# Cross-attention in a decoder layer: the target mask as a scale, five query projections as seven half-size products, and one mask loaded later

## The chip, the cores and the metric

The kernel runs on one core of a Trainium2 chip. The time is the device time of one execution in microseconds (us); below it stands as the median of several runs. A core has five engines, each of which takes its own instructions in order: TensorE (PE: matrix products, with PEld for the loading of weights), VectorE (DVE), ScalarE (ACT), GpSimd (POOL) and SyncE (SP, which here only issues transfers). They wait for each other through semaphores. PE writes its products to PSUM, a small memory of eight banks; DVE and ACT read them from there.

## What is computed

One decoder layer in float32, for 8 positions of 512 rows with 512 features each. Relative-position self-attention over the 8 positions comes first, with a layer norm; then cross-attention to a context of 512 rows with 1024 features, with a layer norm; then a feed-forward layer with 2048 hidden features rounded to an 8-bit format, and a layer norm. The change touches the cross-attention:

```python
src_trans = einsum('bsf,of->bso', src, W_src) + b_src
tgt_trans = einsum('btf,of->bto', tgt, W_tgt) + b_tgt
src_trans = src_trans * src_mask[:, :, None]
tgt_trans = tgt_trans * tgt_mask[:, :, None]
k, v = split(src_trans)            # 8 heads of 64
q = tgt_trans                      # 8 heads of 64
scores = einsum('bthd,bshd->bhts', q, k) / sqrt(64)
scores = where(src_mask[:, None, None, :] == 0, -inf, scores)
attn = softmax(scores, axis=-1)
tgt_update = einsum('bhts,bshd->bthd', attn, v)
out = einsum('btf,of->bto', concatenate([tgt, tgt_update]), W_out) + b_out
```

Both masks are the same array: one row of 512 zeros and ones for each of the 8 positions. A query row whose mask is zero has all scores equal, so its softmax is the plain mean over the unmasked keys.

## The kernel before

The kernel has two parts. The first part does the self-attention for four groups of 128 rows. The order of its products on PE is planned by costs written into the code (`must`, `fill`, `slot`), and between them it works off the projection of the context into keys and values for positions 0 to 5, a generator called `context_work`. These projections use a scheme for 2 x 2 blocks of matrices that needs seven half-size products instead of eight, after Strassen and Winograd; it needs sums of the weight blocks (`sums_of_a`) and of the data blocks (`steps_of_b`). In the same generator `sum_w1` loads blocks of the feed-forward weights `w1`, forms their sums on POOL, and `store_w1` writes them to a DRAM buffer `w1d`; load and store are issued by SP.

The second part goes round by round over the positions, `t` from 0 to 7. PE, DVE, ACT and SP follow the written order. In round `t` stand the attention of position `t`; the output projection of position `t - 1` (`output_of`, again seven products, line 1307); the closing products of the feed-forward of position `t - 2` (`finish`, four steps for four groups of rows, lines 1481 to 1491); the queries of position `t + 1` (`queries`, line 1094); and the hidden layer of position `t - 1` (`hidden_of`, seven products for each of four groups, line 1389). The list `dense` holds all but the attention, each step with a cost. `weave` sets the attention steps (scores, line 1115; attention times values, `av`, line 1216) between them, spaced by these costs.

The softmax runs beside this: `scores` queues small steps for DVE and ACT, and `run` issues some of them ahead of every PE step, in proportion to that step's cost. A score block takes a DVE step that adds the mask and finds the row's minimum (line 1130), an exponential on ACT (line 1140), a division (line 1155) and a transpose (line 1163) on DVE; 16 transfers then arrange the blocks (`move_blocks`, tiles `pb` to `pT`).

`queries` multiplies 512 columns at a time: for each of four output groups four matmuls are summed in one PSUM bank, and DVE then adds the bias and multiplies by `mq` (line 1102). `load` brings one mask row to all partitions, and POOL makes two tiles of it: `mb`, 1e30 where a key is masked, and `mq`, the mask times -1/8. PSUM has a pool of four banks (`ps_b`) for all products but the scores. `hp` is a pool of three tiles (`hs`) for the partial results of `hidden_of`. `ring` holds two slots of seven weight blocks for `hidden_of`, and between them a block of `w_xo` for `output_of`. `load_x1T` brings the input of a position, which `turn_x1` transposes on DVE.

## Time and profile before

| | |
|---|---|
| time, median of 3 runs | 2002.66 us (2002.34 to 2005.05) |
| profiled execution | 2002.95 us, of which the span is 2001.2 us |
| first part | 0 to about 865 us |
| first queries of the second part | 864.7 us |
| rounds 2 to 6 | 132 us each |
| PE busy | 1967.3 us, 98% of the span |
| DVE busy | 1582.2 us, 79% |
| ACT busy | 564.1 us, 28% |
| POOL busy | 228.3 us, 11% |

The profile is one execution as the hardware's profiler recorded it. A line of a timeline gives the start in us, the length, the engine, the line of the code, the operation, the tile written and the tile read, their shapes, and the number of instructions merged into it. In square brackets stands the idle time before it, with the work of another engine that ended it. One matmul call in float32 appears as two instructions; the length of a group includes the run-out of its last one, so the distance between the starts of groups tells the rate. Lines of stretches give, for each engine, the busy time and the number of instructions, then the clock granted to PE as a share of the full clock, the share of time in which the transfer engines were busy, and GB/s. Lines of waits give the waiting engine, tile and line, what it waited for, the total in us, how often, and the longest.

### The profile page before, as it was taken

Reading aid. Unit: us, or ns where it says so; the run is one execution under the profiler, and the core shown is the slowest. Engines: PE = TensorE matmul, PEld = TensorE weight load, DVE = VectorE, ACT = ScalarE, POOL = GpSimd, SP = SyncE. Lnnn points to the kernel's source line nnn. Section 1 sums busy time; section 2 is a strip of 40 time slices with the busy share of each in tenths; the row PEclk is TensorE's granted clock in tenths of the full one; section 3 lists DMA queues with packets and bytes.
Section 4 is the critical chain, followed back from the end, with each engine's and each line's share of the span. In section 5 each row is a group of like instructions: output and inputs, shape, how many; then the busy total and the mean of one; then the engine's idle time right before and its main releaser. Section 6 shows DMA issues by size and latency. Waiting matters only on the chain.

```text
span 2001.2 us, 20415 instructions
## 1 busy us (share of the span) xinstructions
PE 1967.3 (98%) x6936; PEld 1108.4 (55%) x6936; DVE 1582.2 (79%) x2485; ACT 564.1 (28%) x1226; POOL 228.3 (11%) x232
## 2 busy tenths in 40 slices
PE   9999999998999999999999999999999999999998
PEld 4544444444444444443456657566576575676776
DVE  4999999999899989656796785877958868678443
ACT  2111111120111011123235245253252442535322
POOL 0030022002301121122101001002010010000000
PEclk9999999999999999999999999999999999999999
DMA  6635136251342352678598667776877676855621
GB/s 227 226 116 219 42 114 233 77 206 65 102 168 78 120 203 65 166 251 211 167 199 248 149 185 229 153 204 166 187 207 172 165 214 156 232 148 145 204 93 60
DMA packets 248104, 328.87 MB, mean 164 GB/s; under 512 B 85312, under 2 KB 140608, under 8 KB 243776
## 3 DMA queue, kind: packets, MB, share of 16 engines
q1 hardware_dynamic: 229200, 291.09, 51.2%
q10 hardware_dynamic: 17056, 29.66, 4.4%
q0 software_dynamic: 1744, 6.82, 0.9%
q8 instruction: 55, 0.90, 0.2%
q14 instruction: 49, 0.40, 0.1%
HBM read 195.90 MB, written 64.49 MB: 130 GB/s over the span
## 4 chain that ended last, share of the span: by engine, by line
PE 74%; DVE 18%; issue 4%; DMA 2%; ACT 1%; POOL 1%; SPq 0%; ACTq 0%; DVEq 0%; POOLq 0%
PE hx L1389 11%; PE hz L1389 5%; PE pox L1307 5%; PE av L1216 5%; PE s L1115 5%; PE o L1481 5%; PE psq L1094 5%; PE px L697 5%; DVE sc L267 4%; PE po L355 4%; DVE pq L258 4%; PE ps_q L225 3%; PE hy L1389 3%; PE poz L1307 3%; PE ps_k L225 3%
## 5 line engine op out<-in xcount | busy, mean ns | idle before, releaser
L1140 ACT ACTIVATE pe<-pe,nmax 128x512 f32<-128x512 f32 x256 | 182.7, 715 | 190.5 <-DVE nmax L1130 160.5
L1130 DVE CUSTOM_DVE_ANT_0 pe<-s,mb 128x512 f32<-128x512 f32 x256 | 162.8, 683 | 27.5 <-PE s L1115 24.4
L1163 DVE STREAM_TRANSPOSE pb<-pe 128x512 f32<-128x512 f32 x256 | 162.2, 682 | 0.6 <-issue 0.6
L258 DVE TENSOR_TENSOR pq<-qw,k 128x2048 f32<-128x2048 f32 x64 | 152.9, 2388 | 1.2
L322 DVE TENSOR_TENSOR pv<-v,sc 128x2048 f32<-128x2048 f32 x64 | 147.0, 2297 | 6.2 <-ACT v L295 4.5
L267 DVE TENSOR_REDUCE sc<-pq 128x64 f32<-128x2048 f32 x64 | 145.9, 2280 | 1.0
L1115 PE MATMUL s<-kT,qTx 64*128 64x512 f32 x512 | 129.8, 624 | 3.4 <-DVE nmax L1130 3.2
L225 PE MATMUL ps_q<-w_in,xt 128*128 128x512 f32 x256 | 117.7, 603 | 5.2 <-DVE qw L254 5.2
L1216 PE MATMUL av<-pT,vx 128*64 128x512 f32 x512 | 118.3, 604 | 4.2 <-DMA kT<-kd 4.2
L1389 PE MATMUL hx<-x2s,w1r 128*128 128x256 f32 x512 | 119.5, 383 | 0.8 <-DVE hs L1417 0.8
L1155 DVE TENSOR_SCALAR pe<-pe,rden 128x512 f32<-128x512 f32 x256 | 116.7, 498 | 4.5
L225 PE MATMUL ps_k<-w_in,xt 128*128 128x512 f32 x256 | 115.1, 602 | 4.6 <-DMA xt<-in_xT_dram 4.6
L1389 PE MATMUL hx<-x2T,w1r 128*128 128x256 f32 x512 | 118.4, 381 | 0.6 <-ACT hs L1411 0.6
L355 PE MATMUL po<-w_o,aoT 128*128 128x512 f32 x256 | 115.3, 593 | 0.9 <-ACT aoT L371 0.9
L225 PE MATMUL ps_v<-w_in,xt 128*128 128x512 f32 x256 | 114.4, 593 | 0.1
L1481 PE MATMUL o<-w2q,hq 128*128 128x512 fp8e4 x512 | 114.4, 379 | 0.0
L1094 PE MATMUL psq<-x1Ts,w_tgt 128*128 128x512 f32 x256 | 113.8, 596 | 0.6 <-PE av L1216 0.6
L1389 PEld LDWEIGHTS hx<-x2s,w1r 128*128 128x128 f32 x512 | 95.5, 190 | 28.8 <-DVE nmax L1130 14.0
L1389 PEld LDWEIGHTS hx<-x2T,w1r 128*128 128x128 f32 x512 | 96.5, 190 | 20.6 <-issue 6.9
L1418 ACT ACTIVATE hq<-hs 128x512 fp8e4<-128x512 f32 x96 | 60.5, 630 | 145.6 <-DVE hs L1417 145.6
L697 PE MATMUL px<-tx,w 128*128 128x512 f32 x192 | 88.4, 604 | 3.6 <-DVE st L739 3.4
L365 POOL TENSOR_TENSOR r<-r,bo 128x512 f32<-128x512 f32 x32 | 48.9, 1545 | 329.7 <-DMA r<-in_x_dram 327.5
(203 smaller groups left out, 3048.9 us busy)
## 6 DMA issues: line engine op xcount, KB each, us to landing
pT<-pb SPq DMA_DIRECT2D x480, 128.0 KB, 2.4
w1r<-w1d SPq DMA_DIRECT2D x32, 1024.0 KB, 6.9
w1r<-w1d SPq DMA_DIRECT2D x32, 768.0 KB, 5.3
ch<-in_ctxT_dram SPq DMA_DIRECT2D x24, 512.0 KB, 5.8
td<-tx SPq DMA_DIRECT2D x12, 768.0 KB, 4.9
tx<-td SPq DMA_DIRECT2D x12, 768.0 KB, 7.2
r<-in_x_dram SPq DMA_DIRECT2D x32, 256.0 KB, 3.5
x1Ts<-x1d SPq DMA_DIRECT2D x32, 256.0 KB, 6.3
```

The source lines that it names most:

```text
L225: nc.tensor.matmul(ps, lhsT=xt[:, e, :], rhs=w_in[:, e, part * E : (part + 1) * E], start=(e == 0), stop=(e == EC - 1),)
L258: nc.vector.tensor_tensor(pr, qw[:, fs] .rearrange("p (h d) -> p h d", d=D1) .unsqueeze(2) .to_broadcast([P, HH, T, D1]), k_all[j][:, :, f ...
L267: nc.vector.tensor_reduce(sc[j][:, t, g * HH * T : (g + 1) * HH * T], pr.rearrange("p h s d -> p (h s) d"), AX.X, ALU.add,)
L355: nc.tensor.matmul(po, lhsT=aoT[t][:, c * P : (c + 1) * P], rhs=w_o[:, c, :], start=(c == 0), stop=(c == EC - 1),)
L697: nc.tensor.matmul(bank, lhsT=w7[:, a, f, i * P : (i + 1) * P], rhs=b[f], start=start and f == 0, stop=f == HF - 1, skip_group_check=not s ...
L1094: nc.tensor.matmul(ps, lhsT=w_tgt[:, e, o * P : (o + 1) * P], rhs=x1T[t][:, e, :], start=(e == 0), stop=(e == EC - 1),)
L1115: nc.tensor.matmul(ps[:, h, :], lhsT=qT[t, c][half[h], j * P : (j + 1) * P], rhs=kT[t, c][half[h], :], start=True, stop=True,)
L1130: nc.vector.tensor_tensor_reduce(out=pe, in0=ps[:, h, :], in1=mb[t], scale=1.0, scalar=FMAX, op0=ALU.add, op1=ALU.min, accum_out=nmax[:, h ...
L1140: nc.scalar.activation(pe, pe, AF.Exp, bias=nmax[:, h : h + 1], scale=-1.0, accum_out=den[:, h : h + 1],)
L1216: nc.tensor.matmul(av[half[h], :], lhsT=v[t, c][:, s, half[h]], rhs=pT[t, c][:, :, :, s, h].rearrange("p g i q -> p (g i) q"), start=(s == 0),
L1389: nc.tensor.matmul(banks[g, name][:, i], lhsT=w[:, f, i * P : (i + 1) * P], rhs=b[:, f], start=start and f + i == 0, stop=f == 1, skip_gro ...
L1481: nc.tensor.matmul(po, lhsT=rows_of_j, rhs=w2q[:, c, :], start=(c == 0), stop=(c == HC - 1),)
```

## The change

*The mask.* `mq` goes. The queries are no longer multiplied by the mask: `queries` only adds the bias. The DVE step on the scores takes a scale per row, `score_scale`, which is the mask times -1/8, and the sign of `mb` is turned. A masked query row then gets equal exponentials over all 512 keys, masked ones too; as masked values are zero, the division only needs a factor, `row_scale`, which is 1 for an unmasked row and 512 over the number of unmasked keys for a masked one. `count_valid` computes both once, in the setup of the first part. The mask is loaded straight into `mb`.

*The queries of positions 3 to 7* (`FIRST_HALVED`) become seven half-size products, `query_steps`. The sums of the query weights are made in `context_work` with those of `w1`: four more blocks, stored to `wtd`. Three of the sums come into free places of `ring` at the end of `output_of` (`load_wt`), and the second part of a `w1` block that stood there is loaded after the queries instead; the fourth sum takes the place of a quarter of `w_tgt` in round 1 (`load_wt3`). The sums of the data are made by `query_sum` in the `hs` tiles. The results are gathered in the query tiles by ACT (`keep`) and DVE (`add`). Between the products stand the sums for the hidden layer and its first product.

*The mask of position 1* is loaded behind the fourth step of round 0 rather than at its start.

The core of the diff:

```diff
@@ in context_work
                 blocks = [(4 * part + n, f) for n in range(4) for f in range(2)]
+                blocks += [(8 + part, f) for f in range(2)]
...
-                        if i == 1 and m < PAIRS - 1:
+                        if (i == 1 and m < PAIRS - 1) or (i == 0 and m > 0):
                             sum_w1(w7[:, 7], *blocks.pop(0))
@@ load
-            mq = mp.tile([P, S], F32, tag="mq", name=f"mq{t}")
-            nc.sync.dma_start(mq, mask[t].partition_broadcast(P))
             mb[t] = mp.tile([P, S], F32, tag="mb", bufs=2, name=f"mb{t}")
-            nc.gpsimd.tensor_scalar(mb[t], mq, 0.0, MASKED, ALU.is_equal, ALU.mult)
-            nc.gpsimd.tensor_scalar(mq, mq, -1.0 / math.sqrt(D2), None, ALU.mult)
-            return mq
+            nc.sync.dma_start(mb[t], mask[t].partition_broadcast(P))
+            nc.gpsimd.tensor_scalar(
+                mb[t], mb[t], 0.0, -MASKED, ALU.is_equal, ALU.mult
+            )
@@ queries
-            nc.vector.scalar_tensor_tensor(
-                qT[t, o], ps, col(C_BT + o), mq, ALU.add, ALU.mult
+            nc.vector.tensor_scalar(qT[t, o], ps, col(C_BT + o), None, ALU.add)
+        def query_sum(t, i):
...
+            dst, u, w = (
+                (1, b12, b11),
+                (2, b22, query_t[t, 1]),
+                (3, b22, b12),
+                (4, b21, query_t[t, 2]),
+            )[i]
+            nc.vector.tensor_tensor(query_t[t, dst], u, w, ALU.subtract)
+        def query_steps(t):
...
+            def product(name, w, b, start):
+                if start:
+                    query_bank[name] = bank(f"q{name}{t}").rearrange(
+                        "p (i q) -> p i q", i=2
+                    )
+                for f in range(2):
+                    for i in range(2):
+                        nc.tensor.matmul(
+                            query_bank[name][:, i],
+                            lhsT=w[:, f, i * P : (i + 1) * P],
+                            rhs=b[:, f],
+                            start=start and f + i == 0,
+                            stop=f == 1,
+                            skip_group_check=not (start and i == 0),
+                        )
...
+            def keep(r, c, name):
+                for i in range(2):
...
+                    nc.scalar.activation(
+                        target(r, c, i),
+                        query_bank[name][:, i],
+                        AF.Identity,
+                        bias=col(C_BT + 2 * r + i),
+                    )
+            def add(r, c, name):
+                for i in range(2):
+                    y = target(r, c, i)
+                    nc.vector.tensor_tensor(y, query_bank[name][:, i], y, ALU.add)
...
+            def y():
+                product("y", of_w(0, 1), of_x(1, 0), True)
+                keep(0, 0, "y")
+            def x():
+                product("x", of_w(0, 0), of_x(0, 0), True)
+                add(0, 0, "x")
+            def z():
+                product("z", sums_of_w(0), query_t[t, 1], True)
+                keep(1, 1, "z")
+            def x2_():
+                product("x", sums_of_w(1), query_t[t, 2], False)
+                keep(0, 1, "x")
+                query_sum(t, 3)
+            def z2():
+                product("z", sums_of_w(2), of_x(1, 1), False)
+                add(0, 1, "z")
+            def x3():
+                product("x", of_w(1, 0), query_t[t, 3], False)
+                add(1, 1, "x")
+            def x4():
+                product("x", of_w(1, 1), query_t[t, 4], False)
+                keep(1, 0, "x")
+            return sum([of(1.8, f) for f in (y, x, z, x2_, z2, x3, x4)], [])
@@ scores
-                    scale=1.0,
+                    scale=score_scale[:, t, j : j + 1],
...
-                        pe, pe, rden[:, h : h + 1], None, ALU.mult
+                        pe,
+                        pe,
+                        rden[:, h : h + 1],
+                        row_scale[:, t, js[i] : js[i] + 1],
+                        ALU.mult,
+                        ALU.mult,
@@ the rounds
-                mq = load(t + 1) if t + 1 < T else None
...
+                halved = FIRST_HALVED <= t + 1 < T
+                if 0 < t < T - 1:
+                    load(t + 1)
...
-                        3: of(0.0, convert, 1) + of(0.0, turn_v_soon, 1),
+                        3: of(0.0, convert, 1) + of(0.0, turn_v_soon, 1) + of(0.0, load, 1),
...
+                    if halved:
+                        dense += of(0.0, query_sum, t + 1, 0)
                     dense += done[2]
...
+                    if halved:
+                        dense += of(0.0, query_sum, t + 1, 1)
+                        dense += of(0.0, query_sum, t + 1, 2)
                     dense += done[3]
...
+                    if halved:
+                        dense += asked[:5] + sums[0] + sums[1] + asked[5:6]
+                        dense += steps[:1] + sums[2] + asked[6:] + sums[3]
+                        dense += of(0.0, load_w1, (t - 1) * GROUPS + 1, 1)
+                        queried = len(dense)
+                        steps = steps[1:]
+                    else:
+                        dense += asked[:-1] + sums[0] + sums[1] + asked[-1:]
+                        dense += sums[2] + sums[3]
+                        queried = len(dense)
                     dense += steps
```

## The prediction

> **What bounds the kernel now.** I read the engine table first, then the busy slices, then busy time by stretches of 200 us.
>
> ```profile
> PE 1967.3 (98%) x6936; PEld 1108.4 (55%) x6936; DVE 1582.2 (79%) x2485; ACT 564.1 (28%) x1226; POOL 228.3 (11%) x232
> PE   9999999998999999999999999999999999999998
> ...
> DVE  4999999999899989656796785877958868678443
> ...
> 1200.00:1400.00 200.00, 199.94 (x866) 133.50 (x865) 147.23 (x327) 82.55 (x191) 22.98 (x18) 1.00 0.71 188
> ```
>
> In the second half TensorE (PE) is busy 199.94 of 200 us at full clock, so a microsecond off its work, or a microsecond in which it waits, counts in full. VectorE (DVE) has 147 of 200 there, an average that hides where it lags. The timeline of one round of 132 us shows where: PE first, then DVE over the same stretch.
>
> ```profile
> 1289.21 3.63 PE L1481 MATMUL o<-w2q,hq 128*128 128x512 fp8e4 x16
> 1292.68 3.60 PE L1094 MATMUL psq<-x1Ts,w_tgt 128*128 128x512 f32 x8
> 1298.12 10.57 PE L1094 MATMUL psq<-x1Ts,w_tgt 128*128 128x512 f32 x24
> ...
> 1279.60 0.18 DVE L109 RECIPROCAL rs_b<-sd_b 128x4 f32<-128x4 f32 x1 [0.36 <-ACT sd_b L107]
> ...
> 1301.85 0.67 DVE L1068 STREAM_TRANSPOSE vx<-raw 128x512 f32<-128x512 f32 x1
> 1302.44 0.71 DVE L1102 SCALAR_TENSOR_TENSOR qTx<-psq,colv,mq 128x512 f32<-128x512 f32 x1
> ...
> 1305.28 0.74 DVE L1102 SCALAR_TENSOR_TENSOR qTx<-psq,colv,mq 128x512 f32<-128x512 f32 x1
> ...
> 1322.31 0.17 DVE L1152 RECIPROCAL rden<-den 128x2 f32<-128x2 f32 x1 [1.60 <-ACT pe L1140]
> ```
>
> The first query product ends at 1296.2, and DVE empties its bank at 1302.44: 6.2 us late. DVE does not idle from 1279.60 to 1320.7, because four closing steps (`finish`), the normalisation, the transposes and the softmax all fall here. Before, this lag is free: the four products use four banks, and PE goes on.
>
> Last, what a wait of PE costs besides itself: the timeline of PE, and the granted clock (the column after POOL's) in the stretches behind two waits.
>
> ```profile
> 172.36 5.40 PE L697 MATMUL px<-tx,w 128*128 128x512 f32 x8 [2.30 <-DVE st L739]
> 917.44 3.79 PE L1115 MATMUL s<-kT,qTx 64*128 64x512 f32 x8 [2.92 <-DVE nmax L1130]
> 968.43 5.00 PE L1216 MATMUL av<-pT,vx 128*64 128x512 f32 x16 [4.22 <-DMA kT<-kd]
> 488.54 6.06 PE L225 MATMUL ps_q<-w_in,xt 128*128 128x512 f32 x8 [5.20 <-DVE qw L254]
> ...
> 174.00:176.00 2.00, 2.00 (x4) 0.82 (x3) 1.38 (x2) 0.00 (x0) 0.00 (x0) 0.53 0.47 180
> 490.00:492.00 2.00, 2.00 (x3) 0.68 (x2) 2.00 (x3) 0.00 (x0) 0.00 (x0) 0.50 0.00 0
> ```
>
> Undisturbed, these groups take 3.60 (px, ps_q), 1.99 (s) and 3.65 us (av). After a wait of 2.30 to 5.20 us the clock is about half for some 4 us, and PE loses 1.8, 1.8, 1.35 and 2.46 us more.
>
> **The change, part by part.** The sum is made against the profiled execution: span 2001.2, time 2002.95, 0.29 over the median of 2002.66.
>
> *Seven half-size products, positions 3 to 7.* Per position, 16 matmuls of 512 columns become 28 of 256; each is two instructions. In the chain 24 psq instructions take 10.50 us (437.5 ns each) and 16 of hx 3.65 (228 ns). So 32 x 0.4375 = 14.0 us becomes 56 x 0.228 = 12.77: a gain of 1.23 us, 6.2 over five.
>
> *The waits it adds.* `y`, `x`, `z` come first, then a second product is summed into the bank of `x`. It has to wait until DVE has read the first (`add(0, 0, "x")`). Only `z`, 8 x 0.228 = 1.8 us, lies between. In the changed program's order on DVE these two adds stand behind all the work of the lag, plus three query sums. The walk, with times of the round shown:
> - PE: the order puts the output's last product after the scores, so it ends at 1278.62 rather than 1276.7. The end of `o_3` stays at 1292.7; scores 1.92 and three products 5.5 put PE at 1300.1.
> - DVE: `rs_b` comes 2.9 us after that last product, 1281.5. Then reciprocal 0.2, normalisation and transpose 1.5, closing step 2.27, three more pairs 4.4, `x1T` transposes 2.38, first query sum 0.7 (as L148), one score step 0.6, reciprocal and two divisions 1.1: 1294.7. The next division waits until ACT has loaded its table and taken the exponential (1.28 + 0.9 after the score step): 1295.9. Division 1.1, closing step 2.27, two query sums 1.4, four transposes 2.4, closing step 2.24, `vx` transpose 0.6, reciprocal 0.2, three output normalisations 1.5: 1307.6. Two adds of 256 columns (0.34 each, as L1295 at 128x256): 1308.3.
>
> PE waits 1308.3 - 1300.1 = 8.2 us. Behind it in PE's queue stand the four other query products, the hidden layer's first product and two scores: everything. The second wait is that of `x3` for ACT's `keep(0, 1)`, queued behind two exponentials and a table load: 1313.1. At full clock PE would be there at 1312.0, and wait 1.1 us.
>
> The half clock takes the 1.1 us over: with 1.35 to 2.46 us lost, I take 1.95 (the mean of the four is 1.85, and this wait is longer than any), PE reaches `x3` near 1314. So 8.2 + 1.95 - 1.23 = +8.9 us per position; the last has no `vx` transpose (0.6 less). Five: +44. Nothing gives it back: PE is full until the next round, and DVE is idle again before the next lag. Bounds: 7 to 9 us of wait and 1.35 to 2.46 of clock (upwards also the 1.1 us): +35 to +56.
>
> The Trainium skill ("TensorE: Matmul & The Clock Gate", Part 1) puts the return to full clock at about 3.4 us of sustained activity, and lets it fall only after an idle window of that length. The rows here fall already after 2.30 us. From its 3.4 us at half rate one would estimate 1.7 us a wait, 8.5 in all, against the rows' 9.8.
>
> *DVE and ACT load.* Four evictions (737 ns) give way to four sums (0.69) and six half adds (0.34): +1.9 us a round, inside the walk. ACT gets eight half evictions (467 ns), beside 28% load. The second scalar of the division and the pointer scale of the scores: one pointer costs 498 ns (L1155), two 504 to 560 (L113), so 0 to 62 ns; a gain is excluded, as nothing is taken out. I take 0; 0.4 us in the walk is its upper end.
>
> *Weights through the ring.* `load_wt` issues 768 KB as two transfers (0.38 us of SP each), some 40 us before use. Behind them on SP stand four `x1T` loads, wanted a round later. The second part of the next `w1` block goes out only after the queries; ten products (18 us) lie between it and its use, and 6.9 us is its landing. Cost 0; with that cover gone, 6.9 a position. `load_wt3` is one transfer of 256 KB, a round ahead: 0.
>
> *Sums of the query weights, first part of the kernel.* Four more blocks: 16 sums on POOL, 3.5 us a block, 14.1 us beside a POOL busy 133 of 870; eight loads and four stores on SP, where `w1d` stores waited for POOL 44.8 us in 11 cases, with `xt`, `r` and context loads behind. PE waited for a transfer once in this part (2.1 us), for DVE 5.2. So -2 to +5; I take +1. `count_valid`: one matmul (pg: 0.22 us) and six small DVE steps (about 0.18 each) in the 2.12 us that DVE idles before the first `qw`: +0.2.
>
> *Mask.* The score scale replaces `mq`; POOL loses 1.5 us a position, off the path. The mask now lands in `mb`, so SP waits until the previous position's last scores are read; behind it is a `kT` load that waited for PE until 1244.7 anyhow, 5 us after the mask's issue at 1239.5: 0. In round 0 it moves. These rows show what it held:
>
> ```profile
> 896.45 2.32 POOL L967 TENSOR_SCALAR mb<-mq 128x512 f32<-128x512 f32 x1 [26.32 <-DMA mq<-in_mask_dram]
> ...
> 903.10 0.69 ACT L179 ACTIVATE kst<-psk,colv 128x512 f32<-128x512 f32 x1 [10.74 <-DMA kd<-kst]
> ```
>
> POOL waits for the mask with the `kd` store behind it; ACT waits for that store with exponentials behind it; DVE idles 11.1 us for those; PE waits 2.92 at 917 and loses 1.8 by the clock. If all goes: -4.7. The wait at 968 (4.22 + 1.35) could go as well: -10.3; or the moved mask does the same where it is now: 0. I take -4.7, as 968 waits for other transfers.
>
> Sum: 2002.95 + 44 + 1.2 - 4.7 = 2043.5; taken as 2044.
>
> **Rivals.**
> 1. *Faster: DVE is in time.* The gains alone, 6.2 + 4.7 - 1.2, give 1993. For it: 53 us of 200 are idle on DVE, and the hidden layer's seven products, with the same bank summed four times, hardly wait, as the waits of PE say:
>
> ```profile
> PE hx L1389 <- DVE hs L1417: 0.8, 1, 0.8
> ```
>
> It decides if the adds end before PE is done with `z`, 8.2 us earlier than the walk has them. Against: no gap in 41 us of DVE; and the hidden layer puts two products and an attention product between, after the lag is worked off.
> 2. *Half the wait.* If the DVE work is shorter or PE later by some 4 us, a position costs 4 + 1.8 - 1.2 = 4.6: 2002.95 + 23 - 3.5 = 2022.
> 3. *The weights come late as well*: 3 to 7 us more a position, 2060 to 2078. Against: the cover named above.
> 4. *No difference*: gain and short waits (1.2 us a position) cancel, and round 0 keeps its wait: 2003.
>
> **How the numbers follow.** Forecast 0.72, rival 1 0.08, rival 2 0.12, rival 3 0.05, rival 4 0.03. The forecast's own range: +35 to +56, with -10.3 to 0 and -2 to +5, each not at its end at once, 2028 to 2060. Reaching to rival 2, the range is 2018 to 2060. About 0.2% (4 us) is what a measurement can tell from none. Faster 0.08; same 0.04; slower 0.88.
>
> **What would show it.** Right: among PE's waits a line of the query products for DVE `qTx`, about 8 us, five times; a granted clock near 0.5 behind each; rounds of 141 rather than 132 us; no wait at 917. Wrong: five rounds of about 131 us. I am wrong if DVE enters the stretch earlier than 1281.5, if ACT makes it wait where I have none, or if its steps with two scalars cost other than the rows I took.

## The result and the profile after

The changed kernel takes 2038.81 us (median of 4 runs, 2037.17 to 2040.1), the kernel before 2003.03 us beside it (2002.34 to 2005.05): a ratio of 1.0177, with a 95% interval of 1.0159 to 1.0194. It is 1.8% slower; the forecast was 2044 us. The profiled execution took 2039.12 us, with a span of 2037.3.

The engine table and the busy slices of TensorE (PE) in the profile after; the second fence is the row of the stretch from 1200 to 1400 us (busy time of PE, weight loads, DVE, ACT, POOL, then granted clock, DMA share and GB/s).

```profile
PE 1967.5 (97%) x7058; PEld 1137.1 (56%) x7058; DVE 1625.7 (80%) x2522; ACT 581.7 (29%) x1266; POOL 229.5 (11%) x240
...
PE   9999999998999999998999899899899898999998
```

```profile
1200.00:1400.00 200.00, 192.50 (x854) 133.33 (x855) 147.09 (x316) 85.09 (x195) 19.91 (x16) 0.98 0.71 188
```

PE's busy time has not changed in sum (1967.3 us before, 1967.5 now), though the queries are less work. The slices of the second half, all 9 before but the last, now hold 8s, and in the stretch from 1200 to 1400 us PE is busy for 192.50 in place of 199.94 us, at a mean clock of 0.98 in place of 1.00. The waits of PE say what it waits for (us in total, times, longest):

```profile
PE qx L1175 <- DVE qTx L1203: 37.0, 5, 7.5
...
PE s L1255 <- DVE nmax L1270: 3.0, 4, 1.5
...
PE hx L1535 <- DVE hs L1563: 0.8, 1, 0.8
```

The hidden layer's products wait as little as before. The four waits of the scores (`s`) lie in round 0. The line of the query products is new: the query products in bank `x` wait for VectorE's `qTx`, 37.0 us in five waits, one in each round with half-size products. Here is one such round on PE and then, from the same stretch, the end of DVE's work ahead of the add for `x` (start, length, what was done, and in brackets the idle time before it and what ended that).

```profile
1299.09 1.99 PE L1175 MATMUL qy<-x1Ts,w_tgt 128*128 128x256 f32 x8
1300.92 1.89 PE L1175 MATMUL qx<-x1Ts,w_tgt 128*128 128x256 f32 x8
1302.65 1.89 PE L1175 MATMUL qz<-qs,w1r 128*128 128x256 f32 x8
1312.04 3.78 PE L1175 MATMUL qx<-qs,w1r 128*128 128x256 f32 x8 [7.50 <-DVE qTx L1203]
1315.62 1.98 PE L1175 MATMUL qz<-x1Ts,w1r 128*128 128x256 f32 x8
1317.43 1.89 PE L1175 MATMUL qx<-qs,w_tgt 128*128 128x256 f32 x8
```

```profile
1285.89 0.18 DVE L112 RECIPROCAL rs_b<-sd_b 128x4 f32<-128x4 f32 x1 [0.37 <-ACT sd_b L110]
...
1305.98 0.66 DVE L1635 TENSOR_TENSOR o<-o,b2q 128x512 f16<-128x512 f32 x1
...
1308.23 0.71 DVE L1098 STREAM_TRANSPOSE vx<-raw 128x512 f32<-128x512 f32 x1
...
1309.04 2.28 DVE L116 TENSOR_SCALAR x<-x,mvc,rs_c 128x512 f32<-128x512 f32 x3
1311.24 0.75 DVE L1203 TENSOR_TENSOR qTx<-qx,qTx 128x256 f32<-128x256 f32 x2
```

PE is done with `z` at 1304.5 and stands until 1312.04. DVE is not idle from 1285.89 on: the closing of the last output block (from 1305.98), the transpose of the values, the reciprocal and three output normalisations all come before the two adds at 1311.24, which end at 1311.99. PE goes on 0.05 us later. The product behind the wait takes 3.78 us, the one after it 1.98. The granted clock in single microseconds:

```profile
1308.00:1309.00 1.00, 0.00 (x0) 0.00 (x0) 0.97 (x4) 0.66 (x3) 0.00 (x0) 0.98 0.96 209
1309.00:1310.00 1.00, 0.00 (x0) 0.00 (x0) 0.96 (x2) 1.00 (x3) 0.91 (x1) 0.50 0.92 195
...
1315.00:1316.00 1.00, 1.00 (x4) 0.80 (x4) 0.06 (x2) 1.00 (x5) 0.00 (x0) 0.61 0.92 205
1316.00:1317.00 1.00, 1.00 (x7) 0.87 (x5) 0.00 (x0) 1.00 (x4) 0.00 (x0) 1.00 0.94 197
```

It falls to 0.50 at 1309.0, 4.5 us after PE went idle, and is back at about 1315.8, 3.7 us after PE resumed.

A round, from the first query product of one position to that of the next, takes 139.9 us (four rounds, 1159.22 to 1718.90) in place of 132.1. The first part of the kernel, which eleven of the runs below have in common with it, ended between 863.4 and 873.3 us in their profiled executions, so the kernels are compared below also by their **second part**, from the first query product of position 0 to the end of the span, and by this **round**. Before: second part 2001.2 - 864.7 = 1136.5 us, round 132.1. After: 2037.3 - 864.0 = 1173.3 us, round 139.9. Round 0 is taken from the first query product of position 0 to that of position 2, as the queries of position 1 fall into it. Of the 36.8 us of difference, round 0 gives back 2.7 (161.2 in place of 163.9 us), and the five rounds with half-size products cost the rest.

### The profile page after: what moved, and what is told of

The parts are those of the page before. It is cut to its first block, busy times and chain, and to the rows that moved or that the text cites. A ratio compares the mean times of both kernels' runs of the same rounds, so it can differ in the third digit from the quotient of the medians.

```text
span 2037.3 us, 20787 instructions
## 1 busy us (share of the span) xinstructions
PE 1967.5 (97%) x7058; PEld 1137.1 (56%) x7058; DVE 1625.7 (80%) x2522; ACT 581.7 (29%) x1266; POOL 229.5 (11%) x240
## 4 chain that ended last, share of the span: by engine, by line
PE 72%; DVE 21%; issue 2%; DMA 2%; ACT 1%; SPq 0%; POOL 0%; ACTq 0%; DVEq 0%
PE hx L1535 11%; PE px L730 6%; PE hz L1535 5%; PE pox L1452 5%; PE s L1255 5%; PE av L1361 4%; PE po L358 4%; PE ps_q L228 3%; PE ps_v L228 3%; PE ps_k L228 3%; DVE sc L270 3%; PE pz L730 3%; PE psk L174 3%; PE hy L1535 3%; PE poz L1452 3%; DVE pq L261 2%
## 5 line engine op out<-in xcount | busy, mean ns | idle before, releaser
L1270 DVE CUSTOM_DVE_ANT_0 pe<-s,mb,score_scale 128x512 f32<-128x512 f32 x256 | 178.7, 746 | 15.9 <-PE s L1255 14.6
L1295 DVE TENSOR_SCALAR pe<-pe,rden,row_scale 128x512 f32<-128x512 f32 x256 | 132.7, 561 | 4.7
L1563 DVE TENSOR_TENSOR hs<-hz,hs 128x512 f32<-128x512 f32 x32 | 22.1, 690 | 90.8 <-PE hz L1535 87.3
```

The lines of the kernel that those rows point to most:

```text
L1270: nc.vector.tensor_tensor_reduce(out=pe, in0=ps[:, h, :], in1=mb[t], scale=score_scale[:, t, j : j + 1], scalar=FMAX, op0=ALU.add, op1=ALU ...
```

## The experiments

The theory was that of the prediction: VectorE is late at one place, and the second product in `x` is the first work of PE that has to wait for it. The rivals were other causes at the same place (weights, clock, ACT), and other parts of the change. All times are medians beside runs of the kernel before on the same chip.

### Is it VectorE's lateness? Its work left out

```diff
+            if bare:
+                if j == NJ - 1:
+                    side.append((("y", t), 1.0, lambda: None))
+                    for k in range(NJ):
+                        side.append((("y", t), 0.7, lambda k=k: put(t, k)))
+                return
             r = x1[t][:, j, :]
             nc.vector.tensor_tensor(r, r, o16, ALU.add)
             stats_of(sm, mvc[t][:, j % n, :], r, f"c{t}_{j}")
```

Here `bare` holds for positions 0 to 4; the lines behind it only store the output rows as they stand.

> The changed kernel with VectorE's residual sum, statistics, root and output normalisation left out for the first five positions (their output is then stored as it stands before these steps); the eviction of the output blocks stays, TensorE's order is unchanged, and nothing else of VectorE's or ACT's is put in their place. That takes three sums with their statistics (1.55 us each) and three normalisations with the reciprocal (2.4 us) from ahead of the add, 7.0 us, and the root that ACT's copies stood behind. Theory (VectorE is late by 7.5 us at this place, itself and through ACT's root): the wait falls to 0.5 us, 1.5 at most, and the product behind it runs at 1.9 us; 2038.8 - 5 x (7.0 + 1.8) = 1995 us, 1990 to 2003. Rival (a further engine or the exchange of the banks holds the product): waits of 3 us or more stay, 2015 us or more.

1996.7 us (ratio to before 0.997, 0.9959 to 0.9981), round 130.7, second part 1129.9. The query products' waits for DVE in the whole execution, and the place itself:

```profile
PE qx L1175 <- DVE qTx L1203: 1.0, 4, 0.3
```

```profile
1297.31 1.89 PE L1175 MATMUL qz<-qs,w1r 128*128 128x256 f32 x8
1299.45 1.99 PE L1175 MATMUL qx<-qs,w1r 128*128 128x256 f32 x8 [0.25 <-DVE qTx L1203]
```

The five waits of 7.5 us became four of 0.25, the product behind runs in 1.99 us, and 42 us are gone; 44 were expected. The round is 9.2 us shorter, which is the wait (7.25) and the clock's loss behind it (1.85). PE's products are the same in number and shape, so it is not the products, their weights or their bank: it is 7 us of work ahead of an add. The root on ACT went with that work; the next run leaves ACT alone. The round also shows what the half-size products are worth when next to nothing waits: 132.1 - 130.7 = 1.4 us.

### More work ahead of the add

```diff
-                        dense += of(0.0, query_sum, t + 1, 2)
+                        for i in range(5):
+                            dense += of(0.0, query_sum, t + 1, 2)
```

> A sum of the queries' input halves (128x512, 0.60 us from start to start) is made five times in place of once, ahead of VectorE's add for x, in each of the five rounds. Theory (late VectorE): each of the five waits grows by the four sums, 4 x 0.60 = 2.4 us, to 9.9 us, and the time by 12 us: 2051 us, 2048 to 2053. Rival (VectorE has slack there, the wait ends by something else): the waits stay at 7.5 us, 2039 us.

2058.83 us (1.0272, 1.0258 to 1.0286), round 143.2.

```profile
PE qx L1175 <- DVE qTx L1203: 51.5, 5, 10.4
```

The waits grew by 2.9 us: in a row, the four added sums took 0.72 us each from start to start, not 0.60. The round grew by 3.3. So the place passes on every added microsecond of VectorE; the 0.4 us more is clock, which came back later (the product behind the slow one took 2.24 and 2.39 us in the first two rounds, 1.94 and 1.98 without the added sums). The median grew by 20 us, more than 5 x 3.3 = 16.5; in the profiled run 5.5 us lie ahead of the second part, where the kernels do not differ.

### ACT in VectorE's place

If only the add stands in the way, let ACT read the bank that is needed first, and VectorE add the product that nobody waits for.

```diff
             def y():
                 product("y", of_w(0, 1), of_x(1, 0), True)
-                keep(0, 0, "y")
+                add(0, 0, "y")
             def x():
                 product("x", of_w(0, 0), of_x(0, 0), True)
-                add(0, 0, "x")
+                keep(0, 0, "x")
...
-            return sum([of(1.8, f) for f in (y, x, z, x2_, z2, x3, x4)], [])
+            return sum([of(1.8, f) for f in (x, y, z, x2_, z2, x3, x4)], [])
```

> Only who reads the bank of x first is changed: x goes first and ACT keeps it, y comes second and DVE adds it. Theory (VectorE is late, and the second product in bank x stands behind its add): the five waits of 7.5 us at the second product go, since only ACT stands between. VectorE is as late as before, so the next bank that it frees is met: its add of the third product ended 7.2 us of VectorE work after the add that now frees nothing (1311.24 to 1321.1 less the 2.64 us that it idled), about 1318.4, and TensorE would reach the fourth product at about 1313; so a wait of up to 5 us there, with up to 1.8 us of clock. Gain of 2 to 9 us at each of five positions: 2027 us, 2000 to 2030. Rival (the wait is for the summed weights that are loaded or for TensorE's own order, VectorE merely ends at the same time): the wait stays where it is, 2039 us.

2041.36 us (1.0186, 1.017 to 1.0201), round 139.5: no gain, and neither case as written. The wait stayed at the same product, but now for ACT. ACT's timeline at the place, then PE's:

```profile
1302.60 1.28 ACT L110 ACT_TABLE_LOAD   x1
1312.09 0.30 ACT L110 ACTIVATE sd_c<-mvc,eps 128x4 f32<-128x4 f32 x1 [8.20 <-DVE mvc L106]
1312.29 0.82 ACT L1193 ACTIVATE qTx<-qx,colv 128x256 f32<-128x256 f32 x2
```

```profile
1313.16 3.78 PE L1175 MATMUL qx<-qs,w1r 128*128 128x256 f32 x8 [4.87 <-ACT qTx L1193]
...
1320.52 1.99 PE L1175 MATMUL qx<-qs,w_tgt 128*128 128x256 f32 x8 [1.66 <-ACT qTx L1193]
```

In ACT's queue the root of the output's variances (`sd_c`) stands ahead of the copy out of `x`, and it waits 8.20 us for the last statistics of DVE. ACT is busy for 28% of the span, and still as late as DVE. Waits of 4.87 and 1.66 us with their clock took the place of 7.50. The expectation asked which engine reads the bank, not what that engine has to wait for first.

A longer version of the same idea lets ACT make all four reads of `x`, and puts the second product in `z` behind two products of the hidden layer:

```diff
             def x3():
                 product("x", of_w(1, 0), query_t[t, 3], False)
-                add(1, 1, "x")
+                keep(1, 1, "x")
+                add(1, 1, "z")
...
-            return sum([of(1.8, f) for f in (y, x, z, x2_, z2, x3, x4)], [])
+            return sum([of(1.8, f) for f in (x, y, z, x2_, x3, x4, z2)], [])
...
-                        dense += asked[:5] + sums[0] + sums[1] + asked[5:6]
-                        dense += steps[:1] + sums[2] + asked[6:] + sums[3]
+                        dense += asked[:5] + sums[0] + steps[:1] + sums[1]
+                        dense += asked[5:6] + steps[1:2] + sums[2] + asked[6:] + sums[3]
```

> The four products in bank x are read by ACT alone (the third too), VectorE's adds read y and z only, and the second product in z comes last, behind two products of the hidden layer. Theory (late VectorE): no product stands behind an add of VectorE until that has caught up. All of 7.5 us of wait and 1.75 us of clock goes at five positions, 46 us: 2038.8 - 46 = 1993 us, 1990 to 2003 with small waits left, which is below the kernel before (2003.0). Rival (VectorE is short of time in the round as a whole, and its lag is only handed on to the hidden layer's banks): waits of 3 us or more appear in the hidden layer, 2010 to 2030 us.

2058.63 us (1.0272, 1.0258 to 1.0286), round 144.3: 20 us worse than the changed kernel. ACT, then DVE:

```profile
1318.18 1.28 ACT L1280 ACT_TABLE_LOAD   x1 [4.43 <-DVE nmax L1270]
...
1320.90 0.81 ACT L1193 ACTIVATE qTx<-qx,colv 128x256 f32<-128x256 f32 x2
```

```profile
1326.09 0.79 DVE L1203 TENSOR_TENSOR qTx<-qz,qTx 128x256 f32<-128x256 f32 x2 [6.64 <-ACT qTx L1193]
```

The copy of the second sum in `x` (1320.90) stands behind exponentials that wait for DVE's maxima, PE's third product waits for that copy, the third copy waits for PE, and then DVE itself idles 6.64 us for that copy. What was a lag became a chain through three engines. Both expectations missed that; lateness is handed on by each queue that waits for the late engine.

### VectorE's work put off instead of left out

```diff
+            if apart:
+                closing.append(lambda: close_of(t, j, n, po))
+            else:
+                close_of(t, j, n, po)
...
+                    asked[1] = (1.8, lambda f=asked[1][1]: (f(), close()))
```

Here `apart` holds for the fourth output block of the five positions, and `close_of` is VectorE's work on it.

> The changed kernel, with VectorE's closing of the fourth output block (sum with bias, residual, statistics, 2.25 us) and with it the root and the output normalisations (2.4 us) put behind the add for x, in the five rounds with half-size products. TensorE's order is unchanged. Theory (late VectorE): the add ends 4.7 us earlier, about 1307.3 on the clock of the changed kernel's trace, and the wait of 7.5 us becomes about 2.9 us, with up to 1.8 us of clock still lost; the work put behind then makes the fourth product in x wait for the add of the third, about 1.5 us. Gain of 2.5 to 4.5 us a position, 2038.8 - 12 to 22: 2022 us, 2017 to 2028. Rival (the root on ACT or something else than VectorE's order holds the product): waits of 7.5 us stay, 2039 us.

2039.2 us (1.0191, 1.017 to 1.0213), round 140.0: nothing gained. DVE ahead of the add, and PE's waits behind it in a later round:

```profile
1317.08 0.71 DVE L1270 CUSTOM_DVE_ANT_0 pe<-s,mb,score_scale 128x512 f32<-128x512 f32 x1
...
1317.71 0.75 DVE L1270 CUSTOM_DVE_ANT_0 pe<-s,mb,score_scale 128x512 f32<-128x512 f32 x1
...
1319.81 0.79 DVE L1203 TENSOR_TENSOR qTx<-qx,qTx 128x256 f32<-128x256 f32 x2 [0.67 <-ACT qTx L1193]
```

```profile
1459.61 3.78 PE L1175 MATMUL qx<-qs,w1r 128*128 128x256 f32 x8 [5.60 <-DVE qTx L1203]
1464.11 3.78 PE L1175 MATMUL qz<-x1Ts,w1r 128*128 128x256 f32 x8 [0.71 <-ACT qTx L1193]
```

The freed room did not stay free. The planner (`weave` and `run`) spends what is left of its allowance on the next waiting steps: three score steps of about 0.7 us, and the exponentials of ACT with them, came ahead of the copy and the add. The wait shrank to 5.6 us only, a wait of 0.71 us for ACT came behind it, and in three of the five rounds a second group ran at half clock (3.78 us at 1464.11). So this run says nothing against the lag, and much about moving work in a list that a planner fills: leaving the work out with its place in the list kept, as above, was the clean form.

### What the clock costs

```diff
             def z():
-                product("z", sums_of_w(0), query_t[t, 1], True)
+                for n in range(5):
+                    product("z", sums_of_w(0), query_t[t, 1], True, n > 0)
```

> The changed kernel, with the half-size product in z made five times over in place of once (each time from the start, so the last one stands): 4 x 1.73 = 6.9 us of needless work on TensorE, which has to wait for nobody, between the first product in z and the second in x. VectorE's work is unchanged. Theory (the wait ends when VectorE comes to its add, and the slow product behind it is the granted clock): TensorE works through 1304.4 to 1311.3, waits 0.7 us, and the product behind runs in 1.9 us in place of 3.8: 1.8 us less at each of five positions, 2038.8 - 9 = 2030 us, 2027 to 2035. Rival (the product behind the wait is slow for another reason): the times do not change, 2039 us. Second rival (the time that the wait takes is not free): 2039 + 35 = 2073 us.

2041.57 us (1.0196, 1.018 to 1.0213), round 139.4.

```profile
1302.65 1.99 PE L1175 MATMUL qy<-x1Ts,w_tgt 128*128 128x256 f32 x8
...
1306.21 8.80 PE L1175 MATMUL qz<-qs,w1r 128*128 128x256 f32 x40
1315.60 1.99 PE L1175 MATMUL qx<-qs,w1r 128*128 128x256 f32 x8 [0.60 <-DVE qTx L1203]
1317.43 1.89 PE L1175 MATMUL qz<-x1Ts,w1r 128*128 128x256 f32 x8
1320.34 1.99 PE L1175 MATMUL qx<-qs,w_tgt 128*128 128x256 f32 x8 [1.01 <-ACT qTx L1193]
```

Four useless products a round, 6.9 us, would be dear on an engine that is the bound; here they cost nothing (second part 1173.1 us, 1173.3 in the changed kernel, with a round 0 that took 2.0 us more). The second product in `x` starts 12.95 us after `y` (1315.60 - 1302.65), and 12.95 us in the changed kernel (1312.04 - 1299.09): only VectorE sets it. It runs in 1.99 us in place of 3.78, so the slow product was the clock, as the theory had it. But the round gained 0.5 us and not 1.8: PE comes to the third product in `x` earlier and waits 1.01 us there for ACT (1.29 in one of the rounds). The prediction had that wait ("at full clock PE would be there at 1312.0, and wait 1.1 us"); my expectation for this run forgot it.

In an earlier form of the same run the needless products had a bank of their own.

```diff
+                for n in range(4):
+                    product("w", of_w(0, 1), of_x(1, 0), n == 0)
                 product("x", sums_of_w(1), query_t[t, 2], False)
```

> The changed kernel, with four needless half-size products (128x256, 1.73 us each, 6.9 us) put on TensorE ahead of the second product in x, into a bank of their own that nothing reads; their values are left out of the result. VectorE's work is unchanged. Theory (the wait ends when VectorE comes to its add, and the slow product behind it is the granted clock, which fell to 0.50 in the wait): TensorE does the needless work inside the wait, the wait shrinks to about 0.6 us, the first product behind it takes 1.9 us in place of 3.8: 5 x 1.75 = 9 us less in spite of more work, 2030 us, 2027 to 2033. Rival (the product is slow for another reason, such as its weights from the ring, or TensorE's work has no free time there): 2039 us, or up to 2073 if all of the added work counts.

2040.44 us (1.0186, 1.0173 to 1.02), round 140.1.

```profile
1309.01 8.86 PE L1175 MATMUL qw<-x1Ts,w_tgt 128*128 128x256 f32 x32 [2.15 <-DVE o L1637]
1317.71 1.89 PE L1175 MATMUL qx<-qs,w1r 128*128 128x256 f32 x8
...
1450.34 7.17 PE L1175 MATMUL qw<-x1Ts,w_tgt 128*128 128x256 f32 x32 [2.15 <-DVE o L1637]
```

The next free bank had held an output block, so the fill waited 2.15 us for DVE to empty that, and held the second product in `x` back to 14.6 us after `y` (16.3 in the first round shown), in place of 12.95. So this run does not keep PE busy through the wait, as it was meant to. It says something else: in one of the five rounds the clock fell at the end of these 2.15 us (8.86 us for the fill), and in the other four, with the same wait, it did not (7.17 us). The round with the fall took 141.3 us, the three others that can be measured so 139.6 to 139.7: here, where no wait behind it takes the loss over, a fall costs 1.6 us.

### The other parts of the change

Queries as whole products everywhere, all else as changed:

```diff
-        FIRST_HALVED = 3
+        FIRST_HALVED = T
```

> The queries of all positions as whole products again, as in the kernel before; the mask as a scale and a factor, the sums of the target weights in the first part and the later mask stay. Theory (everything lost lies at the second product; the rest gains the 3.4 us of round 0 and no more): 2003.0 - 3.4 = 1999.6 us, 1998 to 2001.5. Rival (the 63 ns that each score step and each division takes longer, 4 us of VectorE in a round, reach the end of the round): slower than before, 2005 us up to 2030 if all eight rounds lose it.

2005.25 us (1.001, 1.0002 to 1.0019; 11 runs). The expected gain of 3.4 us is not there. Round 0 is shorter (159.8 us in place of 163.9), but the later rounds are 133.1 in place of 132.1 (the first of them 132.4), as the rival of the expectation had it. Two short waits, which the kernel before does not have in its rounds, from one round:

```profile
1314.80 1.99 PE L1535 MATMUL hx<-x2s,w1r 128*128 128x256 f32 x8 [0.42 <-DVE hs L1563]
...
1386.74 3.50 PE L1452 MATMUL pox<-w1r,x2s 128*128 128x256 f32 x15 [0.27 <-DVE x2s L1440]
```

To see whether the operands read from a column make them, the same kernel with constants in their place:

```diff
-                    scale=score_scale[:, t, j : j + 1],
+                    scale=1.0,
...
-                        row_scale[:, t, js[i] : js[i] + 1],
-                        ALU.mult,
+                        None,
```

> Whole products of the queries at all positions as in the earlier run with them, and the scale of the score step a constant of 1 and the second factor of the division gone; the mask's scale and factor are so left out of the scores, and nothing else. Theory (the operands read from a column cost 63 ns an instruction, 4 us of VectorE in a round, and 0.5 to 1.1 us of each later round): score step 683 ns and division 498 ns again, rounds of 132.0 us, no waits of the hidden layer for VectorE above 0.8 us in all; 1999 us, 1997 to 2001. Rival (the longer rounds came from the mask's other changes or from noise of the first part): the rounds stay at 132.5 to 133.1 us, 2005 us.

1999.08 us (0.9982, 0.9973 to 0.999; 11 runs), round 132.2, second part 1132.7 against 1137.8. The score steps and divisions of the changed kernel, and then of this one (instructions; busy us, mean ns of one):

```profile
L1270 DVE CUSTOM_DVE_ANT_0 pe<-s,mb,score_scale 128x512 f32<-128x512 f32 x256 | 178.7, 746 | 15.9 <-PE s L1255 14.6
...
L1295 DVE TENSOR_SCALAR pe<-pe,rden,row_scale 128x512 f32<-128x512 f32 x256 | 132.7, 561 | 4.7
```

```profile
L1270 DVE CUSTOM_DVE_ANT_0 pe<-s,mb 128x512 f32<-128x512 f32 x256 | 162.8, 682 | 26.4 <-PE s L1255 25.0
...
L1295 DVE TENSOR_SCALAR pe<-pe,rden 128x512 f32<-128x512 f32 x256 | 117.5, 501 | 4.6
```

746 becomes 682 ns, 561 becomes 501, the short waits are gone, and 6.2 us with them. So the mask as a scale and a factor costs 0.9 us a round where PE otherwise waits for nothing. With the half-size products kept, the same edit:

> The changed kernel with the constant scale and without the second factor (the mask's scale and factor left out of the scores), the half-size products kept. Theory: ahead of the add for x lie one score step and four divisions of the stretch, 5 x 63 ns = 0.3 us, so the wait becomes 7.2 us; elsewhere VectorE catches up in the hidden layer, behind a wait that gives it time, so that the 63 ns cost little there: 5 x 0.3 us and up to 1 us a round in the two rounds without half-size products: 2036 us, 2032 to 2038. Rival (the operands bring VectorE its lag): the wait falls by 2 us or more, 2026 us or less.

2039.06 us (1.0187, 1.0169 to 1.0205), round 140.3 against 139.9. PE's waits, and one of its products behind a long wait:

```profile
PE qx L1175 <- DVE qTx L1203: 35.7, 5, 7.3
```

```profile
1464.00 2.21 PE L1175 MATMUL qz<-x1Ts,w1r 128*128 128x256 f32 x8
```

Here the later rounds gain nothing: the waits went from 7.5 to 7.3 us, and no later round is shorter by more than 0.1 us. The short waits of the kernel with whole products do not occur in the changed kernel, whose hidden layer waits for VectorE once, 0.8 us; that the long wait gives VectorE time to catch up fits this but is not shown by itself. The 0.25 us off each long wait went to the clock, which came back later: the second product in `z`, 1.94 to 2.33 us in the changed kernel, took 2.21 to 2.88 us here. So the two prices do not add up in these rounds. Round 0 is another matter: it took 159.2 us in place of 161.2, and of its four waits for score maxima one of 0.3 us is left. In the profiled kernels with the later load it took 159.8 to 164.0 us in the nine that read columns, and 159.0 to 159.3 in the three that do not.

Last the mask's load. The changed kernel with the load of position 1 at the start of round 0 again:

```diff
-                if 0 < t < T - 1:
+                if t < T - 1:
                     load(t + 1)
...
-                        3: of(0.0, convert, 1) + of(0.0, turn_v_soon, 1) + of(0.0, load, 1),
+                        3: of(0.0, convert, 1) + of(0.0, turn_v_soon, 1),
```

> The changed kernel with the mask of position 1 loaded at the start of round 0 again. Theory (the later load took 2.7 to 4 us out of round 0): round 0 is 161.2 us in the changed kernel, from the first query product of the second part to the first of the next position, and 163.9 us in the kernel before; here 163.9 us again, with the wait of 2.9 us before a score product, and 2041.5 us, 2040 to 2044. Rival (the load's place means nothing, the shorter round comes from the mask's way): round 0 stays at 161 us, 2039 us.

2042.12 us (1.0196, 1.0182 to 1.0209), round 0 163.2 in place of 161.2 us, with a wait before a score product:

```profile
918.63 1.13 PE L1255 MATMUL s<-kT,qTx 64*128 64x512 f32 x4 [2.75 <-DVE nmax L1270]
```

The two intervals overlap (1.0159 to 1.0194 for the changed kernel), and 163.2 us lies within the 159.8 to 164.0 that round 0 took in the profiled kernels with the later load and the columns, so neither decides. The stretch up to the first query product of position 1 does: 71.3 us in each of the twelve profiled kernels with the later load, 74.6 here, 77.2 in the kernel before. And the kernel before with nothing changed but this (`load` keeps the masked scale under the position's number, and the queries look it up):

```diff
-                mq = load(t + 1) if t + 1 < T else None
+                if 0 < t < T - 1:
+                    load(t + 1)
...
-                        3: of(0.0, convert, 1) + of(0.0, turn_v_soon, 1),
+                        3: of(0.0, convert, 1) + of(0.0, turn_v_soon, 1) + of(0.0, load, 1),
```

> The kernel before with one thing of the change: the mask of position 1 is loaded behind the fourth piece of round 0 in place of at its start; mask, queries and score steps are those of before. Theory (the later load takes the wait of 2.9 us with its clock loss out of round 0, and in the kernel with whole products and all else of the change the longer score steps and divisions gave it back at 0.5 to 1.1 us in each later round): round 0 about 4 us shorter than before, the later rounds 132.0 us as before; 2003 - 4 = 1999 us, 1997 to 2001. Rival (round 0 became shorter through the score steps that no longer need the masked queries, not through the load): 2003 us, no change.

1998.36 us (0.9975, 0.9966 to 0.9985; 10 runs): faster than both kernels, and 0.25% below the kernel before. Round 0 is 159.0 in place of 163.9 us, the later rounds 132.1. All waits of PE for score maxima in this kernel, and POOL's mask step, which in the kernel before had stood 26.32 us:

```profile
PE s L1118 <- DVE nmax L1133: 0.3, 1, 0.3
```

```profile
929.43 1.93 POOL L969 TENSOR_SCALAR mb<-mq 128x512 f32<-128x512 f32 x1
```

## Why the prediction was right, and where it was not

- **The wait for the add of `x`** carried the result: predicted 8.2 us, measured 7.50 four times and 6.98 at the last position (the one with less work ahead, as said). Two of its terms were off and partly cancelled: the exponential that DVE was to wait for was in time, as ACT had loaded its table ahead of it (1.2 us too much), and three output normalisations took 2.28 us, not 1.5 (0.8 too little). Shown by leaving the work out, and by the dose.
- **The clock** was put at 1.95 us a wait less 1.1 for the ACT wait that it takes over, so 0.85 net. Measured: the product lost 3.58 - 1.73 = 1.85 us from start to start, the ACT wait is 1.0, and a round without the clock loss is 0.5 us shorter.
- **The gain of the products** was 1.23 us a position; without waits the round is 1.4 us shorter.
- **Sum of a round**: predicted +8.9, measured +7.8. Over five positions that is 5.5 us too high. Round 0 was 2.0 us too low (below), the first part 1.9 too high (+1.2, measured -0.7): 5.4 together, about the 5.2 by which 2044 lay above the result. That the account closes to 0.2 us is luck: in profiled kernels that do not differ there, round 0 took 159.8 to 164.0 us and the first part 863.4 to 873.3.
- **The pointer operands** at 0: this step was wrong. Each instruction took 63 ns more, the upper bound given, and in the kernel with whole products that was 0.9 us a round. In the changed kernel it cost 0.25 us in each long wait, which the clock took back, and nothing else in the later rounds; there "I take 0" was right by luck. In round 0 it cost: see the next point.
- **Round 0** at -4.7: alone it is -4.9 (163.9 to 159.0), in the changed kernel -2.7. Up to the first query product of position 1 both are 5.9 us shorter (71.3 for 77.2). The wait of 2.92 us at 917 went as said; behind that stretch four waits of 0.2 to 1.5 us for score maxima stand in the changed kernel. With constants in place of the columns one of 0.3 us is left, so it was the columns that took part of the gain back. The wait before the attention product at 968 stayed (4.48 us at 963.81), as said.
- **Weights from the ring, sums of the weights, mask of later rounds** at 0, +1 and 0: PE has no wait for the ring in the five rounds, and the second part started at 864.0 in place of 864.7, which tells nothing of +1, as the first part varied by 10 us. The reading that PE waited for a transfer once in the first part left out 4.6 us for `xt` at its very start, ahead of all that the change added.
- **Rival 1** had nearly the right price: with the adds in time the kernel takes 1996.7 us, where 1993 was worked out. Its condition, 8.2 us less of work ahead, was what failed. **Rivals 2 to 4** did not occur.

## What to carry to other kernels

Splitting a product into parts that share an accumulator turns an eviction that was free into one that the bound engine waits for, so look at how late the evicting engine is at that very place, not at its average load (80% here, and 7.5 us late). Another engine for the eviction helps only if nothing ahead in that engine's queue waits for the late one. And test the parts of a bundle alone: here the smallest of the three, one load four steps later, was worth 4.4 us by itself, while the mask's columns cost 0.9 us a round and the half-size products 7.8 as they stood.

## What was not expected of the hardware

- A column operand in place of a constant in the score step cost 63 ns on a 128x512 instruction (683 to 746 ns), and nothing else of that instruction changed. A second column in the division cost as much (498 to 561); a second multiplication came with it, and no run parts the two.
- The clock's fall does not go by the wait's length alone. It fell 4.5 us into a wait of 7.50. Of waits near 2 us, equal ones ended differently: 2.15 us in the run with the fill, one fall in five; in the run with VectorE's work left out, a score group of four took 1.13 us behind a wait of 1.86 (at 942.23) and 2.08 behind one of 1.85 (at 995.71); and behind the 2.75 us at 918.63 above, 1.13 us is full speed. Waits of 0.60 and 1.01 us left it alone. The Trainium skill ("TensorE: Matmul & The Clock Gate", Part 1) describes windows of about 3.4 us that are free-running, so that the point of a change depends on where in the window the first matmul falls. Equal waits with different ends fit that, and so does the return, 3.7 us after PE resumed; that a wait of 1.85 us can be enough does not fit a whole idle window of that length, and the windows themselves no run here shows.
- On a PE that must wait, useless matmuls are free and keep the clock up. They gained only 0.5 of the 1.8 us, as the next wait was already there.
